# A new order string, a memset moved to a later step and stores by smaller pieces in a one-core attention and mixture-of-experts kernel

## The chip, the core and the metric

The kernel runs on one core of one Trainium2 chip. The metric is the device time of one execution in microseconds (us), lower is better. The kernel before was timed in three runs; their median is the number that the change is held against.

## The reference

The input is x with 4 batches of 1024 tokens of 128 features, in fp32. Two blocks follow each other, each added to its input (cut to what matters):

```
n = layernorm(x)
Q, K, V = silu(n@Wq), silu(n@Wk), silu(n@Wv)          # 8 heads of 16
scores = (Q K^T + rel_bias[i - j]) / 4, causal, keys that are all 0 masked
x = x + (silu(scores) @ V) * silu(n@Wu)               # no softmax
n = layernorm(x)
gates = softmax over the 2 largest of n@w_gate^T      # 8 experts
x = x + sum_e gates[e] * ((n @ w_in[e]^T) @ w_out[e]^T)
```

## The kernel before

**Work and groups.** The tokens are cut into groups: seven of 512 tokens (g0 to g6, four tiles of 128) and, at the end, two of 256 (g7 and g8). Groups 2b and 2b+1 belong to batch b; g7 and g8 are the second half of batch 3.

**An order written out by hand.** All instructions come from generators, and each `yield` ends a step. The string `ORDER` has 424 letters; each letter runs the next step of one lane, and the instructions of that step are queued on their engines (TensorE = PE, VectorE = DVE, ScalarE = ACT, GpSimd = POOL, SyncE = SP for DMAs) in the order in which they are written. Each engine works through its own queue in that order; an instruction that must wait holds up everything behind it on its engine, and no other engine. The lanes, with the names that the text uses for their steps:

- P and Q, `prepare`: the two halves of a batch, eight steps each. P1 to P3 make the normalised, transposed input; P4 the keys, P5 the queries, P6 the mask of keys, P7 the values (into `vps`), P8 U. For batch 0 (`layernorm_T`) P1 is statistics on DVE and a power on POOL, P2 the scaling, P3 PE transposes. For the others (`layernorm_cols`) P1 is the statistics, P2 is a transpose on DVE (L276) and three DMAs on SP that write the statistics to DRAM (L277) and read them back as rows for all partitions (L297, L301), and P3 two POOL operations (L305, L306).
- S, `attend`: one unit of scores of 512 columns. PE multiplies into four PSUM banks (L492), then DVE adds the relative bias (L511) and ACT applies silu (L514), or ACT does both where the bias is one constant (L519). The banks come from a ring of seven that nearly all PE work shares.
- W, `weigh`: the product of the oldest waiting unit with V (L470). The last W of a group starts its `finish`.
- C, D, E, `finish`: F1 transposes the result back, F2 to F4 are a layernorm like P1 to P3, F5 the gate logits, F6 to F14 choose two experts on small tiles, F15 writes the gates to DRAM and reads them back broadcast (L628), M0 to M3 multiply a tile of tokens by its eight gates (L635).
- X, Y, Z, `experts` for g0 to g6: X0 to X3, one tile each, 64 matmuls and one DVE addition (L650). For g7 and g8 `experts_then_gates`: for each of two tiles a and b are two products with ACT (L672) and DVE (L676), c three DVE additions (L683 to L685).
- G, `fold`: w_in times w_out of one expert. K, `constants`: K1 is the far bias, K2 and K3 the diagonal tiles of the bias (a POOL select L245 and a DVE copy L249), K4 a ranking, K5 the clearing of `vps[1]`.

Before the first letter, `load_all` issues the loads and the POOL memsets, among them the clearing of `vps[0]` (L169), V's room of batches 0 and 2, 128 x 2048 elements. On SP it loads x, the bias tables, and, behind a wait for a small table that goes through DRAM (`ext`), the rest of x and all expert weights.

**Stores.** `store` issues one DMA to `out` on SP. In `experts` it is called once for a group, after X3; in `experts_then_gates` once for a group, after its last tile.

Of the kernel before, what the change touches and what calls it, by code (L numbers as in the profile page):

```python
# [24 lines left out]
TPB = SB // P  # L25
# [15 lines left out]


ORDER = (
    "PPQPQKPPQKPKSPSPSQQSWWSWGSWQPWSQWSPSCSWQPSCCQKWGSPWPSWWSWPKQSWGSWSWSCWSWPSWPSGDSQQDPQWSCPP"
    "WWSWQWSQDWSSCESCDWPEPCSCWQWEDCSWPCSWCQDSWDCSWDDDCPGSPPWQCDSQWSWSGWESGWPSWSWSDEWECQEDPEDEEC"
    "GDQWWSXSWSQCXECSCEXSECQWSCEXPWPWSDEDQPCQWSDDWDSYDSWQEESWDCYCCYCDCSWWWESCYCSPCWCCSZDCQWSEDZ"
    "SDEWPEQQWSEZSDWWDQDCDQSDCDWZDSDCXCSEWEWEWCCESWEECXXEESQWDSEWDDXSEDEYCSEDDWWDSCCYDCCCSCDCDY"
    "CSCYCDWCDESDWWEDDSZDWWEDWDEYEEYEYYZECZEEECEYEECZXEYEXEEZCZZZXZXZ"
)


# [1 line left out]
def preln_silu_attention_moe(  # L53
# [14 lines left out]
    nc = tc.nc  # L68
# [19 lines left out]
    def misc():  # L88

        return ps_s.tile([P, SB], F32, tag="bank", name="bank")  # L90

    def product(out, stationary, moving, start=True, stop=True):


        for q in range(0, P, 32):
            nc.tensor.matmul(  # L96
                out[q : q + 32, :], stationary[:, q : q + 32], moving, start=start, stop=stop
            )
# [4 lines left out]
    def load_x(b, blk):  # L103
        t0 = blk * TPB
        nc.sync.dma_start(
            xs[b][:, t0 : t0 + TPB, :],
            x[b, blk * SB : (blk + 1) * SB, :].rearrange("(i p) d -> p i d", p=P),
        )
# [15 lines left out]
    def load_w(i, w):  # L124
        nc.scalar.dma_start(wcat[:, i, :], w)

    def load_near(par, to, src, pitch, n):
        nc.sync.dma_start(
            near[:, par, :, to : to + n],
            bass.AP(src.tensor, src.offset, [[1, P], [2 * pitch, NQ], [1, n]]),  # L130
        )

    def load_all():

        pt = misc()
        for i in range(HEAT):
            product(pt[:, :P], ident, ident)

        load_x(0, 0)
        nc.scalar.dma_start(rb[:, NPAD - NR :], rel_biasT)  # L140
        load_w(1, wk)
        load_near(0, FAR, rel_biasT, NR, MAXLEN)

        nc.vector.memset(one, 1.0)
        nc.scalar.activation(one, one, AF.Silu)
        nc.vector.tensor_copy(
            rb[:, : NPAD - NR], rb[:, NPAD - NR : NPAD - NR + 1].to_broadcast([H, NPAD - NR])
        )
        nc.scalar.dma_start(ext[:, :], rb)
        load_w(0, wq)  # L150
        load_x(0, 1)
        load_near(1, FAR, rel_biasT[1:2, :], NR, MAXLEN)

        load_near(0, FAR - P, ext[0:1, FAR - P :], NPAD, P)
        load_near(1, FAR - P, ext[1:2, FAR - P :], NPAD, P)
        load_w(2, wv)
        load_w(3, wu)
        nc.gpsimd.memset(wgT, 0.0)

        nc.gpsimd.memset(ones8, 1.0)  # L160
        nc.gpsimd.affine_select(
            out=ones8, in_=ones8, compare_op=ALU.is_ge, fill=0.0,
            base=0, pattern=[[-HD, H]], channel_multiplier=1,
        )
        nc.gpsimd.affine_select(
            out=ones8, in_=ones8, compare_op=ALU.is_ge, fill=0.0,
            base=HD - 1, pattern=[[HD, H]], channel_multiplier=-1,
        )
        nc.gpsimd.memset(vps[0], 0.0)  # L169
        nc.gpsimd.memset(euler, EULER)  # L170
        for st in stats:
            nc.gpsimd.memset(st, 0.0)
        nc.scalar.dma_start(wgT[:, :E], w_gateT)

        for n in range(2, B * NB):
            load_x(n // NB, n % NB)
        for e0 in range(0, E, 2):

            if e0 % 4 == 0:
                room = gpool.tile([P, 2, 2, 2, NC, D], F32, tag="wide", name=f"w_in_out_{e0}")  # L180
            both = room[:, e0 // 2 % 2]
            for t, w in zip((both[:, 0], both[:, 1]), (w_in, w_outT)):
                nc.sync.dma_start(t, w[e0 : e0 + 2].rearrange("e (c p) d -> p e c d", p=P))
            experts_in.append(both)
# [31 lines left out]
    vps = [cpool.tile([P, NT, 2, NQ, 2, HD], F32, tag=f"vp{i}", name=f"vp{i}") for i in range(2)]  # L216
# [9 lines left out]

    def constants():


        pt = misc()  # L230
        nc.tensor.matmul(
            pt[:, :H], rb[:, :1].to_broadcast([H, P]), ident[:H, :H], start=True, stop=True
        )
        for par in range(2):
            nc.scalar.copy(
                near[:, par, :, : FAR - P],
                pt[:, :H].rearrange("p (k q) -> p q k", q=2)[:, par, :]
                .unsqueeze(2).to_broadcast([P, NQ, FAR - P]),
            )
        nc.vector.tensor_scalar(cscaled, pt[:, :H], SCALE, None, ALU.mult)  # L240
        yield

        for par in range(2):
            diag = near[:, par, :, TAB - P : TAB]
            nc.gpsimd.affine_select(  # L245
                out=diag, in_=diag, compare_op=ALU.is_ge, fill=NEG,
                base=P - 1, pattern=[[0, NQ], [-1, P]], channel_multiplier=-1,
            )
            nc.vector.tensor_copy(near[:, par, :, TAB:], diag)  # L249
            yield  # L250

        nc.gpsimd.iota(
            rank, pattern=[[0, TPB], [-1, E]], base=E, channel_multiplier=0,
            allow_small_or_imprecise_dtypes=True,
        )
        yield
        nc.gpsimd.memset(vps[1], 0.0)
        yield
# [278 lines left out]
    def finish(g, b, t0, nt, gated):  # L537
# [82 lines left out]
        if g in DIRECT:  # L620
            lanes["XYZ"[g % 3]].append(experts_then_gates(b, t0, nt, x2T, gates))
            yield
            return
# [6 lines left out]
            gates_d[g].rearrange("r j -> (r j)").partition_broadcast(P),  # L630
        )
        lanes["XYZ"[g % 3]].append(experts(b, t0, wide_g))
        yield
        for i in range(nt):
# [5 lines left out]
    def experts(b, t0, gated):  # L640

        y = xs[b][:, t0 : t0 + TPB, :]
        for i in range(TPB):
            pt = misc()
            for e in range(E):
                product(
                    pt[:, :D], gated[:, i, e, :], wfold[:, e, :],
                    start=(e == 0), stop=(e == E - 1),
                )
            nc.vector.tensor_tensor(y[:, i, :], pt[:, :D], y[:, i, :], ALU.add)  # L650
            if i == TPB - 1:
                store(b, t0, TPB, y)
            yield

    def experts_then_gates(b, t0, nt, x2T, gates):

        EH = SB // D
        y = xs[b][:, t0 : t0 + nt, :]
        for i in range(nt):

            both = spool.tile([P, 2 * EH, D], F32, tag="both", name="both")
            gy, other = both[:, : EH + 1, :], both[:, EH + 1 :, :]
            for e0 in (EH, 0):
                pt = misc()
                product(
                    pt, x2T[:, i, :], wfold[:, e0 : e0 + EH, :].rearrange("p e d -> p (e d)")
                )
                for e in range(EH):
                    ye = pt[:, e * D : (e + 1) * D]
                    gate = gates[:, i, e0 + e : e0 + e + 1]  # L670
                    if e0:
                        nc.scalar.activation(  # L672
                            other[:, e, :] if e < EH - 1 else gy[:, EH, :], ye, AF.Copy, scale=gate
                        )
                    else:
                        nc.vector.scalar_tensor_tensor(  # L676
                            gy[:, e, :], ye, gate,
                            other[:, e, :] if e < EH - 1 else y[:, i, :],
                            ALU.mult, ALU.add,
                        )  # L680
                yield
            half = EH // 2
            nc.vector.tensor_tensor(gy[:, :half, :], gy[:, :half, :], gy[:, half:EH, :], ALU.add)  # L683
            nc.vector.tensor_tensor(gy[:, 0, :], gy[:, 0, :], gy[:, EH, :], ALU.add)
            nc.vector.tensor_tensor(y[:, i, :], gy[:, 0, :], gy[:, 1, :], ALU.add)  # L685
            if i == nt - 1:
                store(b, t0, nt, y)
            yield

    def store(b, t0, nt, y):  # L690
        nc.sync.dma_start(
            out[b, t0 * P : (t0 + nt) * P, :].rearrange("(i p) d -> p i d", p=P), y[:, :nt, :]
        )
# [10 lines left out]
    lanes["Q"] = [prepare(b, 1) for b in range(B)]  # L704
    lanes["G"] = [fold()]
    lanes["K"] = [constants()]

    def step(lane):
# [52 lines left out]
```

## Time and profile before

| | us |
|---|---|
| median of three runs | 277.42 |
| lowest and highest | 276.55, 277.86 |
| the profiled execution's own time | 276.35 |
| its span, from first to last instruction | 274.6 |
| PE busy in the span | 264.8 |
| DVE busy | 229.8 |
| ACT busy | 194.0 |
| POOL busy | 88.6 |

The profile is of one execution, 1.75 us shorter in span than in time. PE matmuls are pipelined and their ends are modelled, so a busy PE can still be slow inside; the starts of its instructions are exact. "Idle before" is time in which an engine did nothing before a group of instructions, and what it names is what ended the idle time. The TensorE clock was granted in full throughout (1.000).

### The profile page before, as it was taken

Reading aid. Unit: us, or ns where it says so; the run is one execution under the profiler, and the core shown is the slowest. Engines: PE = TensorE matmul, PEld = TensorE weight load, DVE = VectorE, ACT = ScalarE, POOL = GpSimd, SP = SyncE. Lnnn points to the kernel's source line nnn. Section 1 sums busy time; section 2 is a strip of 40 time slices with the busy share of each in tenths; the row PEclk is TensorE's granted clock in tenths of the full one; section 3 lists DMA queues with packets and bytes.
Section 4 is the critical chain, followed back from the end, with each engine's and each line's share of the span. In section 5 each row is a group of like instructions: output and inputs, shape, how many; then the busy total and the mean of one; then the engine's idle time right before and its main releaser. Section 6 shows DMA issues by size and latency. Waiting matters only on the chain.

```text
span 274.6 us, 10777 instructions
## 1 busy us (share of the span) xinstructions
PE 264.8 (96%) x4694; PEld 145.2 (53%) x4694; DVE 229.8 (84%) x594; ACT 194.0 (71%) x316; POOL 88.6 (32%) x101
## 2 busy tenths in 40 slices
PE   7799999999999999999999999999998999999993
PEld 7344443344444234444465347565675776775872
DVE  5597656569976977999989898999899998898994
ACT  2568998879899898889768866575965467684030
POOL 7410136600544712372024241351360343111010
PEclk9999999999999999999999999999999999999999
DMA  5899930330004032272080483217022621845022
GB/s 176 214 301 287 290 128 5 117 117 2 0 5 124 35 77 84 81 300 91 5 309 2 123 333 97 79 41 284 31 82 97 256 80 43 308 143 211 5 60 60
DMA packets 33315, 34.88 MB, mean 127 GB/s; under 512 B 4068, under 2 KB 29676, under 8 KB 32372
## 3 DMA queue, kind: packets, MB, share of 16 engines
q1 hardware_dynamic: 32516, 33.89, 38.3%
q8 instruction: 37, 0.61, 0.9%
q10 hardware_dynamic: 752, 0.31, 0.4%
q14 instruction: 10, 0.08, 0.1%
HBM read 31.74 MB, written 2.45 MB: 124 GB/s over the span
## 4 chain that ended last, share of the span: by engine, by line
PE 85%; DVE 8%; POOL 2%; issue 2%; ACT 1%; POOLq 0%; DVEq 0%
PE bank L96 31%; PE bank L492 29%; PE av L470 22%; DVE w L511 3%; DVE gated L635 2%; PE bank L541 2%; POOL rstd L325 1%; PE bank L569 1%; POOL vp L169 1%; DVE den L608 1%; ACT w L519 1%; DVE attended L479 0%; ACT w L514 0%; POOL xn L330 0%; DVE near L249 0%
## 5 line engine op out<-in xcount | busy, mean ns | idle before, releaser
L511 DVE TENSOR_TENSOR w<-bank,near 128x512 f32<-128x512 f32 (+2 forms) x220 | 116.5, 589 | 18.0 <-PE bank L492 15.0
L514 ACT ACTIVATE w<-w 128x1024 f32<-128x1024 f32 (+2 forms) x110 | 98.2, 915 | 40.5 <-DVE w L511 37.8
L492 PE MATMUL bank<-qT,kT 32*128 32x512 f32 (+3 forms) x864 | 91.0, 483 | 1.4 <-DVE x L650 0.8
L519 ACT ACTIVATE w<-bank,cscaled 128x512 f32<-128x512 f32 (+3 forms) x136 | 70.2, 604 | 10.4 <-PE bank L492 5.9
L470 PE MATMUL av<-w,vp 128*32 128x512 f32 (+3 forms) x864 | 74.0, 454 | 0.4 <-DVE turned L276 0.3
L492 PEld LDWEIGHTS bank<-qT,kT 32*128 32x128 f32 x864 | 39.7, 184 | 39.5 <-DVE w L511 14.9
L96 PE MATMUL bank<-wfold,gated 128*32 128x128 f32 x1792 | 53.9, 273 | 0.3 <-issue 0.3
L96 PEld LDWEIGHTS bank<-wfold,gated 128*32 128x32 f32 x1792 | 48.3, 110 | 9.2 <-issue 4.6
L470 PEld LDWEIGHTS av<-w,vp 128*32 128x32 f32 x864 | 23.2, 109 | 34.6 <-issue 26.3
L635 DVE TENSOR_TENSOR gated<-gated,x2T 128x1024 f32<-128x1024 f32 x28 | 35.8, 1288 | 0.9 <-DMA gated<-gates_d 0.9
L289 POOL TENSOR_TENSOR stats<-rs,mhalf 128x4 f32<-128x4 f32 x13 | 13.2, 1019 | 46.8 <-DVE rs L288 44.0
L96 PE MATMUL bank<-xnT,wcat 128*32 128x512 f32 x192 | 24.3, 597 | 0.5 <-ACT xnT L338 0.4
L605 POOL TENSOR_TENSOR ex<-euler,d 128x4 f32<-128x4 f32 (+1 forms) x9 | 9.6, 1061 | 41.0 <-DVE d L603 37.0
L406 POOL TENSOR_TENSOR vp<-v,kmask 128x256 f32<-128x256 f32 x16 | 9.8, 632 | 31.8 <-ACT v L404 31.8
L305 POOL TENSOR_TENSOR mean<-attended,mean 128x512 f32<-128x512 f32 x7 | 9.3, 1324 | 19.8 <-DMA mean<-stats_d 19.8
L672 ACT ACTIVATE both<-bank,gates 128x128 f32<-128x128 f32 x16 | 4.5, 375 | 14.9 <-DVE gates L619 11.0
L305 POOL TENSOR_TENSOR mean<-xT,mean 128x512 f32<-128x512 f32 x6 | 7.7, 1283 | 20.4 <-DMA mean<-stats_d 20.4
L96 PEld LDWEIGHTS bank<-xnT,wcat 128*32 128x32 f32 x192 | 5.3, 109 | 13.3 <-issue 5.2
L371 ACT ACTIVATE kT<-bank,sel 128x512 f32<-128x512 f32 x16 | 11.0, 690 | 0.2 <-PE bank L96 0.2
L306 POOL TENSOR_TENSOR x2T<-mean,x2T 128x512 f32<-128x512 f32 x7 | 9.8, 1402 | 0.6
L284 DVE BATCH_NORM_STATS2 stats<-x 128x6 f32<-128x256 f32 x26 | 9.8, 418 | 0.1
L96 PEld LDWEIGHTS bank<-w_in_out 128*32 128x32 f32 x256 | 7.0, 110 | 4.5 <-DVE w L511 2.4
(87 smaller groups left out, 204.4 us busy)
## 6 DMA issues: line engine op xcount, KB each, us to landing
gated<-gates_d SPq DMA_DIRECT2D x7, 2048.0 KB, 8.2
mean<-stats_d SPq DMA_DIRECT2D x13, 256.0 KB, 3.6
x<-in_L_attn_x SPq DMA_DIRECT2D x8, 256.0 KB, 6.4
w_in_out<-in_L_ffn_w_in SPq DMA_DIRECT2D x4, 512.0 KB, 7.4
w_in_out<-in_L_ffn_w_out SPq DMA_DIRECT2D x4, 512.0 KB, 7.5
xT<-in_L_attn_x_T SPq DMA_DIRECT2D x8, 256.0 KB, 4.4
x2T<-stats_d SPq DMA_DIRECT2D x7, 256.0 KB, 3.7
out<-x SPq DMA_DIRECT2D x7, 256.0 KB, 2.3
```

Of the source, the lines that this page charges most:

```text
L96: nc.tensor.matmul(out[q : q + 32, :], stationary[:, q : q + 32], moving, start=start, stop=stop)
L284: nc.vector.bn_stats(st[:, 3 * i : 3 * i + 6], src[:, i : i + 2, :].rearrange("p i d -> p d i"))
L289: nc.gpsimd.tensor_tensor(st[:, TPB * 3 : TPB * 4], rs, mhalf, ALU.pow)
L305: nc.gpsimd.tensor_tensor(mean, srcT, mean, ALU.subtract)
L306: nc.gpsimd.tensor_tensor(dst, mean, dst, ALU.mult)
L371: nc.scalar.activation(kT[:, par, s0 : s0 + SB], pk, AF.Silu, scale=sel[:, par : par + 1])
L470: nc.tensor.matmul(acc[k * 32 : (k + 1) * 32, nt * P - n : nt * P], vp[:, j, par, k, :, :].rearrange("p q c -> p (q c)"), w[:, k, c : c + ...
L492: nc.tensor.matmul(ps[k][:, c : c + n], kT[k * 32 : (k + 1) * 32, par, j * P : (j + 1) * P], qT[k * 32 : (k + 1) * 32, lo : lo + n], start ...
L511: nc.vector.tensor_tensor(w[:, k, :nn], ps[k][:, :nn], near_of(k, parts), ALU.add)
L514: nc.scalar.activation(w[:, k : k + 2, :nn], w[:, k : k + 2, :nn], AF.Silu, scale=SCALE)
L519: nc.scalar.activation(w[:, k, lo:hi], ps[k][:, lo:hi], AF.Silu, bias=cscaled[:, h : h + 1], scale=SCALE,)
L635: nc.vector.tensor_tensor(wide_g[:, i], wide_g[:, i], x2T[:, i : i + 1, :].to_broadcast([P, E, P]), ALU.mult)
```

## The change

The clearing of `vps[0]` is no longer issued in `load_all`, but as the first instruction of K1. `experts` stores after X1 and after X3, two tiles each time; `experts_then_gates` stores every tile by itself. `ORDER` is a different string with the same 424 letters, each letter as often as before; 85 of the 424 places hold the same letter. The computation and its instructions stay the same, but for nine more stores.

```diff
 ORDER = (
-    "PPQPQKPPQKPKSPSPSQQSWWSWGSWQPWSQWSPSCSWQPSCCQKWGSPWPSWWSWPKQSWGSWSWSCWSWPSWPSGDSQQDPQWSCPP"
...
-    "CSCYCDWCDESDWWEDDSZDWWEDWDEYEEYEYYZECZEEECEYEECZXEYEXEEZCZZZXZXZ"
+    "PPQQPKKPQPQQPKSPSSSWPSGWSWPWQPSQWPSWSCWCQSPPQSKCWWSCWWPSWSSWCQSWSWQKSWSWPCSWPSGWSCQQSDPWWD"
...
+    "DCDYSDCYCDEWESDWESWDDEWWZDWYEEYEYZECZEEECEYEEXEYEZEEYZCZCZZZXZXX"
 )
...
-        nc.gpsimd.memset(vps[0], 0.0)
         nc.gpsimd.memset(euler, EULER)
...
     def constants():
 
+        nc.gpsimd.memset(vps[0], 0.0)
 
         pt = misc()
...
-            if i == TPB - 1:
-                store(b, t0, TPB, y)
+            if i % 2:
+                store(b, t0 + i - 1, 2, y[:, i - 1 :])
             yield
...
-            if i == nt - 1:
-                store(b, t0, nt, y)
+            store(b, t0 + i, 1, y[:, i:])
             yield
```

More of the change, by code (lines that the diff above doesn't have):

```diff
@@ L43 @@
 ORDER = (
-    "PPQPQKPPQKPKSPSPSQQSWWSWGSWQPWSQWSPSCSWQPSCCQKWGSPWPSWWSWPKQSWGSWSWSCWSWPSWPSGDSQQDPQWSCPP"
-    "WWSWQWSQDWSSCESCDWPEPCSCWQWEDCSWPCSWCQDSWDCSWDDDCPGSPPWQCDSQWSWSGWESGWPSWSWSDEWECQEDPEDEEC"
-    "GDQWWSXSWSQCXECSCEXSECQWSCEXPWPWSDEDQPCQWSDDWDSYDSWQEESWDCYCCYCDCSWWWESCYCSPCWCCSZDCQWSEDZ"
-    "SDEWPEQQWSEZSDWWDQDCDQSDCDWZDSDCXCSEWEWEWCCESWEECXXEESQWDSEWDDXSEDEYCSEDDWWDSCCYDCCCSCDCDY"
-    "CSCYCDWCDESDWWEDDSZDWWEDWDEYEEYEYYZECZEEECEYEECZXEYEXEEZCZZZXZXZ"
+    "PPQQPKKPQPQQPKSPSSSWPSGWSWPWQPSQWPSWSCWCQSPPQSKCWWSCWWPSWSSWCQSWSWQKSWSWPCSWPSGWSCQQSDPWWD"
+    "SPWSWGPSDCWQSEWSDQECPCPSWEQGCQDSWSCDGCCWSWPDCDQSDDWWSEWEEEPDSWSPWDSGWDSGCWDGSXDQSCWQQCSWXE"
+    "WPESCWCEESCXPWSWQPDDECWSEXECDEQDYWSDYDSYCCQQCSCCWCSCWDPPECQSWWPESEDWPCSYDWCCQSWSEWDQQWDSWD"
+    "SDZWDCZESEPZSDWSDXSWWDEQQCDSWZDCCSWSECWECSEEEXCESWEEXWDWQESDWSDYDXCCEESCEDCDCWSWDCYDCSCDDC"
+    "DCDYSDCYCDEWESDWESWDDEWWZDWYEEYEYZECZEEECEYEEXEYEZEEYZCZCZZZXZXX"
 )
```

## The prediction

> **What bounds the kernel now.** I read the page's busy line first, then the chain of waits, the groups by form, the waits, and last the timeline at both ends and around the first batch change. PE is busy nearly throughout, and the chain that ended last lies on PE from 13 us on:
>
> ```profile
> span 274.6 us, 10777 instructions
> PE 264.8 (96%) x4694; PEld 145.2 (53%) x4694; DVE 229.8 (84%) x594; ACT 194.0 (71%) x316; POOL 88.6 (32%) x101
> PE 85%; DVE 8%; POOL 2%; issue 2%; ACT 1%; POOLq 0%; DVEq 0%
> ```
>
> But busy is not full speed. From the starts of matmuls in the timeline I took what each step costs when nothing holds it (lower quarter of its kind): an S step 1.07 us, a W step 0.88, an expert tile of 64 matmuls 1.77, a projection 0.86 to 0.90. All steps: 73 S and 73 W make 142, 28 expert tiles 49, the projections 29, fold, direct products, transposes and logits 24, in all 243.9 us. The first transpose starts at 7.39 and the last matmul ends at 270.39: 263.0. So some 19 us are PE held up, 11 of them in sixteen steps that each took over 0.25 us too long. Both strings hold the same steps; the order can touch only those 19 us, the 7.4 before and the 4.2 behind.
>
> What holds PE is the ring of seven banks, emptied by DVE and ACT:
>
> ```profile
> L511 DVE TENSOR_TENSOR w<-bank,near 128x512 f32<-128x512 f32 x156 | 95.9, 680 | 11.4 <-PE bank L492 11.2
> L514 ACT ACTIVATE w<-w 128x1024 f32<-128x1024 f32 x78 | 82.1, 1058 | 40.5 <-DVE w L511 37.8
> L635 DVE TENSOR_TENSOR gated<-gated,x2T 128x1024 f32<-128x1024 f32 x28 | 35.8, 1288 | 0.9 <-DMA gated<-gates_d 0.9
> ```
>
> Started back to back, an addition takes 0.60 us, a silu of 1024 columns 0.96, a gate multiplication 1.12. An S step with four additions costs DVE 2.4 us for PE's 1.07; such steps must be spread between steps that are PE's alone.
>
> **The tail.** The chain's last pieces:
>
> ```profile
> 255.31 15.08 PE bank L96 x440
> 270.39 0.02 issue
> 270.41 0.29 DVE x L650
> 270.70 0.34 DVE both L683
> ...
> 271.14 0.30 DVE both L684
> 271.44 0.02 issue
> 271.47 0.29 DVE x L685
> ```
>
> PE runs without a gap to 270.39, X3 of g6. Behind it DVE does X3's addition and then the three of g8's last tile (letter Z), to 271.76; the last store and its landing take the rest to 274.6. The new string ends XX, with that Z ahead of both: three additions, 1.06 us (271.76 less 270.70), go before the last matmul. Is DVE then late by itself? In the window 250 to 275 it is busy 19.92 us and has almost no gap from 250.2 to 269.9. But M3 of g5 (1.12) and F14 of g7 (0.26) now stand ahead of the last W, not behind it: DVE has 1.4 us less to do after that W. So X3 stays PE's, and the tail gives **-1.06**.
>
> **The start.** The lines that carry it:
>
> ```profile
> 1.80 1.80 POOL L169 MEMSET vp<- 128x2048 f32 x1
> 2.48 1.58 DVE L146 COPY rb<-rb 8x256 f32<-8x256 f32 x1 [1.57 <-DMA rb<-in_L_attn_rel_bias]
> 7.77 0.76 DVE L316 BATCH_NORM_STATS2 st<-x 128x6 f32<-128x256 f32 x2 [0.67 <-DMA x<-in_L_attn_x]
> 10.79 1.22 POOL L245 TENSOR_SCALAR_AFFINE_SELECT near<-near 128x512 f32<-128x512 f32 x2
> 10.93 0.66 PE L337 MATMUL bank<-ident,xn 128*128 128x128 f32 x4
> ```
>
> The memset ends at 3.60, and POOL then idles 1.10 until DVE's statistics: nothing on POOL waited for it. Its cost may be on DVE: the copy of 256 elements took 1.58 us beside it, while the same operation on 512 (L249) took 0.83 and 0.41. The Trainium skill, SBUF — State Buffer, section "SBUF: two separate sides", says that DVE and GpSimd share a port pair as an exclusive lock held for a whole instruction. By that rule the copy would end 1.2 us sooner, and so would the small table, the loads behind it, and P1: up to -1.2. By the row, the second half of x lands at 7.77 whatever DVE does, and the steps behind it set when scores start. I take 0 at the start. In its new place the memset stands on POOL after Q's scaling (10.82): 10.8 to 12.6, and delays the two selects and the copy by 1.8. That copy then ends near 14.1 instead of 12.29. In the new string the queries come after Q3's transposes (10.93), so the second half of the keys is ready near 13.9 anyway: 0.2 is lost at most, and the first scores start near 14.9 instead of 13.21 with 1.8 us more of projections done (5.5 instead of 3.7 us of PE work). Bounds -1.2 to +1.8, value 0.
>
> **Stores.** Nine more on SP:
>
> ```profile
> L691 SPq DMA_DIRECT2D out<-x x9: 372/389/425, 153.6 to 271.8; - x9
> DMA to landing us min/median/max: 2.3/2.3/2.3
> ```
>
> That is 9 x 0.39 = 3.5 us of SP, which issues little after 60 us. A store waits for an addition that DVE does before any transpose that a later SP transfer needs, so it holds nothing up. Against splitting speaks the Trainium skill, DMA: Bandwidth & Descriptors, section "Anatomy of one DMA": a fixed cost of about 2.0 us each (fitted on the GpSimd path). Nine of those in a row would be 18 us; by the row they overlap other work, and only the last landing counts, which is of two tiles before and after. Value 0; ends -0.3 (less queued behind) and +0.4 (one issue more).
>
> **The order inside.** I walked along both strings with a balance: each step adds its DVE (and, in a second balance, ACT) time and takes off its PE time, never below zero. What exceeds 4 us counts as PE waiting: seven banks are 1.75 S steps, at 2.4 us of DVE each. Before: 3.5 us (M0 and M1 of g0, M3 of g1, M1 of g3). After: 2.0, of which 1.6 in the opening, where S steps come three in a row. With limits of 3.5 and 4.5 it is 7.8 to 5.7 and 2.0 to 1.1. I take **-1.5**; ends +1 and -3, since the balance finds only part of the 19.
>
> **Leads.** The layernorms through DRAM have a latency of their own. The first:
>
> ```profile
> 33.20 0.67 SPq L277 DMA_DIRECT2D stats_d<-turned  x1
> 36.36 0.38 SPq L297 DMA_DIRECT2D mean<-stats_d  x1
> ...
> 40.35 1.27 POOL L305 TENSOR_TENSOR mean<-xT,mean 128x512 f32<-128x512 f32 x1 [4.36 <-DMA mean<-stats_d]
> 41.69 1.29 POOL L306 TENSOR_TENSOR xnT<-mean,xnT 128x512 f32<-128x512 f32 x1
> ```
>
> DVE's transpose ended at 33.17, POOL at 42.98: 9.8 us; the others took 7.9 to 9.3 where POOL was free. Before, P4 of this half came at 44.5, 1.5 us later than needed. In the new string P2 comes earlier (18.3 instead of 23.1 us of PE work) but finds SP still issuing expert weights and x transposed until 31.6, so the keys' input is ready near 42.6, while PE reaches P4 (27.6 us of work, about 12.4 behind the clock) near 40. It stands 2.6 us. ACT, which is busy 26.7 of the 30 us from 32 to 62 and paces that stage, loses only about 1.6, and part returns by the second group: **+0.7**. Other leads shrink too, in PE work between transpose and use: g5 13.9 to 9.1, g4 16.0 to 10.3, batch 2 first half 12.2 to 10.4, g0 32 to 9.7. With DVE 0.3 to 2.5 us behind PE there (the balance), most just hold: **+0.3**.
>
> **Sum.** -1.06 + 0 + 0 - 1.5 + 0.7 + 0.3 = -1.6. The profiled execution took 276.35 (span 274.6 and 1.75 around it), 1.07 below the median; I take the difference from the median: 277.42 - 1.6 = 275.8.
>
> **Rivals.**
> - The balance is half of it: the new string also spreads what the balance doesn't see, and saves 3 us inside. For: 11 us sat in single steps. Against: the opening packs five S steps closer. -3.1: 274.3. Chance 0.18.
> - Slower by late layernorms: DVE runs 2 to 3 us behind PE where the new leads are shortest (as it did at batch 2's P2, 3 us). Then PE stands at P4 of batch 1 in full (2.6), and, at a lag of 3, at F5 of g5 (9.05 + 3 - 9.1 = 3), of g0 (8.1 + 3 - 9.7 = 1.4) and at batch 2's P4 (8.7 + 3 - 10.4 = 1.3); behind each, S steps and their DVE and ACT work start late. At a lag of 2 us it is 2.6 + 2.0 + 0.4 + 0.3 = 5.3; less the tail's 1.06 and the balance's 1.5 that leaves +2.7: 280.1. It decides from where the waits pass 2.6 us in sum, which P4 alone reaches if nothing of it returns. Chance 0.23.
> - The parts cancel: the first batch's loss eats the tail's gain, the balance means nothing. 277.4. Chance 0.12.
>
> **How the numbers follow.** About 0.5%, 1.4 us, is what a measurement of this kernel can tell from no change. My forecast has 0.47 (own range 274.6 to 276.9), 0.29 of it beyond 0.5%. Faster 0.29 + 0.18 = 0.47; same 0.18 + 0.12 = 0.30; slower 0.23. The range 273.0 to 279.4 leaves out the ends of the first two rivals, somewhat under 2 in 10.
>
> **What would show it.** Tail: X3's addition is the last DVE instruction, 0.3 us after the last matmul. Start: L146 well under 1 us, scores from about 14.9. First batch change: PE stands before P4's product near 40 to 43. Inside: fewer S steps far over 1.07 us. Wrong: PE waiting for POOL x2T L306 or xnT at several places, or a last matmul later than 270.4.

## The result, and the profile after

The changed kernel took 280.53 us in the median of 22 runs, the kernel before, run beside it, 276.97: a ratio of 1.0116 (95% interval 1.0089 to 1.0142). It is slower by 1.2%, and above the range predicted. The ratio leaves out runs over 1.5% above their kernel's fastest, six of the changed kernel's 22 and its first traced execution among them, so the lines of "after" are of a later execution of the same kernel (280.37 us, span 278.7; that set of runs gave 1.0123, 1.0079 to 1.0166). In its code L228 is the moved memset and L690 the store.

The head of the page of after, and its chain:

```profile
span 278.7 us, 10800 instructions
PE 268.3 (96%) x4694; PEld 147.1 (53%) x4694; DVE 232.5 (83%) x594; ACT 194.6 (70%) x316; POOL 90.5 (32%) x101
PE 79%; DVE 10%; ACT 5%; issue 3%; POOL 2%; DVEq 0%; POOLq 0%
```

PE is busy 3.5 us longer with the same instructions, and 6% of the chain have gone from PE, most of it to ACT and DVE. Between the first transpose and the last matmul PE needs 243.9 us of undisturbed steps in both kernels; what it takes beyond that I call its excess, whether PE waits, runs slowly or is at half clock. It was 19.1 us before and is 23.9 here.

**The opening.** The timeline of after (start, duration, instruction, idle time before it):

```profile
3.16 0.28 DVE L146 COPY rb<-rb 8x256 f32<-8x256 f32 x1 [2.25 <-DMA rb<-in_L_attn_rel_bias]
...
9.78 2.76 DVE L330 TENSOR_SCALAR xn<-x,st,rstd 128x128 f32<-128x128 f32 x3 [1.15 <-POOL rstd L325]
...
10.61 1.93 DVE L240 TENSOR_SCALAR cscaled<-bank 128x8 f32<-128x8 f32 x1
10.66 1.80 POOL L228 MEMSET vp<- 128x2048 f32 x1
...
12.60 0.47 PE L337 MATMUL bank<-ident,xn 128*128 128x128 f32 x1 [1.39 <-DVE cscaled L240]
```

L146 is free of the memset and takes 0.28 us instead of 1.58. The price stands below: the memset follows POOL's own scaling at once, and DVE's third scaling (inside the 2.76 us) lasts until it ends, 2.18 us where it took 0.44 before. L240, of 8 columns, stands behind that scaling on DVE and ends with it (1.93, before 0.18). The last of Q3's transposes, which needs the third scaling, waits 1.39 us; the profile names L240, which ended at the same time. The same stretch by windows of 2 us (busy time of PE, PEld, DVE, ACT, POOL, then the granted clock):

```profile
10.00:12.00 2.00, 0.79 (x7) 0.34 (x3) 2.00 (x4) 0.69 (x1) 2.00 (x2) 1.00 0.67 144
12.00:14.00 2.00, 1.41 (x9) 0.53 (x13) 1.37 (x3) 0.59 (x1) 1.65 (x3) 0.65 1.01 267
14.00:16.00 2.00, 2.00 (x16) 0.45 (x12) 0.00 (x0) 1.00 (x2) 0.00 (x0) 0.50 1.20 314
16.00:18.00 2.00, 2.00 (x36) 0.69 (x28) 1.21 (x3) 1.54 (x4) 0.00 (x0) 1.00 1.19 288
```

After the gap PE runs at half clock until 16.01 us: products of 0.86 us take 1.71. The first scores start at 17.26 us, against 13.21 before. Not all of that stays lost. The keys of batch 1 (P4) wait in the new order for their input, which a layernorm through DRAM brings:

```profile
42.64 1.92 PE L96 MATMUL bank<-xnT,wcat 128*32 128x512 f32 x16
```

The input was ready at 42.59. With the memset in its old place (a_memset_back, below) PE stands 1.60 us there and starts at 42.22. In these two executions, then, only 0.4 us of what the memset does to the opening reaches beyond P4.

**Inside.** Near 104 us, the layernorm of g2 and the mask of keys of batch 2 (P6, L387), timeline of after:

```profile
104.34 1.28 POOL L305 TENSOR_TENSOR mean<-attended,mean 128x512 f32<-128x512 f32 x1 [3.22 <-DMA mean<-stats_d]
104.39 1.28 DVE L587 TENSOR_TENSOR oh<-lg,m 128x32 f32<-128x32 f32 x1
...
105.70 1.27 POOL L306 TENSOR_TENSOR x2T<-mean,x2T 128x512 f32<-128x512 f32 x1
105.77 1.25 DVE L616 TENSOR_TENSOR oh<-oh,g 128x32 f32<-128x32 f32 x1
...
107.16 0.69 DVE L387 TENSOR_TENSOR nz<-kT 128x512 bf16<-128x512 f32 x1
...
107.90 0.26 PE L96 MATMUL bank<-ones,nz 128*32 128x8 bf16 x16 [1.72 <-DVE nz L387]
```

L587 and L616 took 0.19 and 0.18 us in the median before. Each started just after a POOL instruction and ended with it; the two lost 2.2 us, L387 came late, PE stood 1.72. The windows behind it again show half clock:

```profile
104.00:108.00 4.00, 2.28 (x43) 0.79 (x40) 3.75 (x9) 3.78 (x8) 2.55 (x2) 1.00 0.24 83
108.00:110.00 2.00, 2.00 (x24) 0.57 (x22) 1.01 (x7) 0.00 (x0) 0.00 (x0) 0.54 0.05 8
110.00:112.00 2.00, 2.00 (x16) 0.52 (x16) 1.83 (x4) 0.45 (x1) 0.00 (x0) 0.60 0.51 131
```

Instructions of DVE that lie beside such a POOL instruction and are over 0.15 us longer than their kind: about 10 before, 6.6 us too long in sum; about 14 after, 10.4 us (L240 counted).

**The tail and the stores.** The chain's last pieces, and the stores' line:

```profile
274.69 0.30 DVE both L684
274.99 0.02 issue
275.02 0.29 DVE x L685
275.31 0.48 DVE x L650 x2
```

```profile
L690 SPq DMA_DIRECT2D out<-x x18: 332/386/392, 139.8 to 275.8; - x18
DMA to landing us min/median/max: 1.5/2.5/6.5
```

The last matmul ends at 275.43, X3's addition is the last thing DVE does, and the span ends 3.2 us after the matmul instead of 4.3.

### The profile page after: what moved, and what is told of

It reads as the page before. It is cut to its first block, busy times and chain, and to the rows that moved or that the text cites. A ratio compares the mean times of both kernels' runs of the same rounds, so it can differ in the third digit from the quotient of the medians.

```text
span 281.6 us, 10800 instructions
## 1 busy us (share of the span) xinstructions
PE 270.6 (96%) x4694; PEld 147.3 (52%) x4694; DVE 232.5 (83%) x594; ACT 194.7 (69%) x316; POOL 90.9 (32%) x101
## 3 DMA queue, kind: packets, MB, share of 16 engines
HBM read 31.74 MB, written 2.45 MB: 121 GB/s over the span
## 4 chain that ended last, share of the span: by engine, by line
PE 77%; DVE 8%; DMA 5%; ACT 5%; SPq 2%; issue 1%; DVEq 0%
PE bank L96 27%; PE bank L492 25%; PE av L470 22%; ACT w L519 3%; DVE w L511 3%; DMA w_in_out<-in_L_ffn_w_out 3%; DMA ext<-rb 2%; SPq L105 2%; ACT w L514 2%; PE bank L541 2%; DVE gated L635 1%; DMA rb<-in_L_attn_rel_bias 1%; DVE both L676 1%; SPq L128 1%; DVE gates L619 1%
## 5 line engine op out<-in xcount | busy, mean ns | idle before, releaser
L519 ACT ACTIVATE w<-bank,cscaled 128x512 f32<-128x512 f32 (+3 forms) x136 | 70.0, 611 | 10.3 <-PE bank L492 8.8
L470 PE MATMUL av<-w,vp 128*32 128x512 f32 (+3 forms) x864 | 76.7, 465 | 0.0
L289 POOL TENSOR_TENSOR stats<-rs,mhalf 128x4 f32<-128x4 f32 x13 | 13.6, 1045 | 61.8 <-DVE rs L288 44.6
L96 PE MATMUL bank<-xnT,wcat 128*32 128x512 f32 x192 | 26.6, 657 | 0.4 <-ACT xnT L338 0.4
L605 POOL TENSOR_TENSOR ex<-euler,d 128x4 f32<-128x4 f32 (+1 forms) x9 | 10.5, 1162 | 25.8 <-DVE d L603 25.8
L305 POOL TENSOR_TENSOR mean<-attended,mean 128x512 f32<-128x512 f32 x7 | 9.7, 1393 | 20.8 <-DMA mean<-stats_d 20.8
L96 PEld LDWEIGHTS bank<-xnT,wcat 128*32 128x32 f32 x192 | 6.3, 119 | 13.8 <-issue 7.3
L305 POOL TENSOR_TENSOR mean<-xT,mean 128x512 f32<-128x512 f32 x6 | 7.7, 1284 | 17.1 <-DMA mean<-stats_d 17.1
L291 POOL TENSOR_TENSOR attended<-attended,xT 128x512 f32<-128x512 f32 x7 | 9.4, 1342 | 0.0
```

The source lines that it names most:

```text
L96: nc.tensor.matmul(out[q : q + 32, :], stationary[:, q : q + 32], moving, start=start, stop=stop)
L289: nc.gpsimd.tensor_tensor(st[:, TPB * 3 : TPB * 4], rs, mhalf, ALU.pow)
L305: nc.gpsimd.tensor_tensor(mean, srcT, mean, ALU.subtract)
L470: nc.tensor.matmul(acc[k * 32 : (k + 1) * 32, nt * P - n : nt * P], vp[:, j, par, k, :, :].rearrange("p q c -> p (q c)"), w[:, k, c : c + ...
L519: nc.scalar.activation(w[:, k, lo:hi], ps[k][:, lo:hi], AF.Silu, bias=cscaled[:, h : h + 1], scale=SCALE,)
L605: nc.gpsimd.tensor_tensor(ex, euler[:, :nt], d, ALU.pow)
```

## The experiments

Ratios are to the kernel before, run on the same chip, with the 95% interval.

**The parts by themselves.** The new string and stores, memset in its old place (a_memset_back):

```diff
+        nc.gpsimd.memset(vps[0], 0.0)     # in load_all, where it was
...
-        nc.gpsimd.memset(vps[0], 0.0)     # in K1
```

> New order and new stores, the clearing of vps[0] back in load_all. Theory lock: the three L330 of Q2 take 1.0 us together, Q3's transposes start near 11.0, no half clock in the first 25 us, 3 to 4.5 us less than the changed kernel: ratio to before 0.995 to 1.002. Theory order: nothing of note returns, ratio to before 1.008 to 1.014; L146 is again 1.58 us.

The old kernel with only the memset moved to K1 (b_memset_k1), and with only the new stores (b_stores):

> Old order and old stores, the clearing of vps[0] at K1. Theory lock: K1 follows Q2 in the old order too, so L330 of Q2 is held as well, Q3's transposes start near 13 instead of 10.93, PE idles some 2 us and may lose its clock: 2 to 4.5 us more than before, ratio 1.007 to 1.016. Theory order: within 0.4% of before, since nothing waits on POOL there.

> Old order, old place of the memset, new stores (two tiles, or one). Theories lock and order: within 0.3% of before, as 9 more issues of 0.39 us stand on a queue that is mostly idle. A theory that the stores cost: SP's issues push a layernorm's transfers or the broadcast of gates back, ratio 1.004 or more.

The changed kernel once more (a_again), on the same chip:

> The changed kernel once more, for a second trace and a time beside the others. Theory lock (the memset of vps[0], now at K1, holds DVE's scaling of the second half of x through the port that DVE and POOL share; PE then idles over 1 us and runs at half clock for some us): L330 of Q2 takes over 2 us again, the granted clock falls below 1 before 25 us, ratio to before 1.010 to 1.015. Theory order (the loss lies in the new order of steps, wherever the memset is): the same ratio, but the opening ends (first W, g0.0) less than 2 us later than before's for the PE work done by then, and the loss lies later.

Measured: a_memset_back 1.0091 (1.0061 to 1.0121), b_memset_k1 1.0086 (1.0060 to 1.0111), b_stores 0.9995 (0.9972 to 1.0017). The stores cost nothing that shows. The memset alone, and the string with the stores, each cost nearly a percent, and all together only 1.2%: on top of the string the memset adds 0.25%, uncertain by 0.4. Timeline of b_memset_k1, the old string:

```profile
10.72 2.76 DVE L330 TENSOR_SCALAR xn<-x,st,rstd 128x128 f32<-128x128 f32 x3 [1.16 <-POOL rstd L325]
...
11.61 1.80 POOL L228 MEMSET vp<- 128x2048 f32 x1
...
13.54 0.33 PE L337 MATMUL bank<-ident,xn 128*128 128x128 f32 x1 [1.39 <-DVE cscaled L240]
```

It is the same picture as in after, so the place of the memset makes it, not the string. In a_memset_back there is no such gap (0.92 us remain), and PE waits later instead, at P4 of batch 1's first half:

```profile
42.22 1.92 PE L96 MATMUL bank<-xnT,wcat 128*32 128x512 f32 x16 [1.60 <-POOL xnT L306]
```

In after PE comes to this product later by more than that (42.64) and does not wait. So most of what the opening wins is waited away at P4, which fits that the parts don't add up.

**Other places and shapes of the memset**, in the old kernel: eight memsets of 256 elements at K1 (b_memset_pieces), and one in K3, behind the second select (b_memset_k3).

```diff
+        for i in range(NT):
+            nc.gpsimd.memset(vps[0][:, i], 0.0)
```

> Old order and stores, the clearing of vps[0] at K1 but as eight memsets of 256 elements instead of one of 2048. Theory lock (what holds DVE is one long POOL instruction that has the shared port until it ends): the third L330 of Q2 waits for one piece at most (0.3 us), Q3's transposes start before 11.7 instead of 13.2, and most of the 0.86% of the single memset at K1 is gone: ratio 0.998 to 1.004. Rival (POOL's queue is what is late: the selects of K2 behind the same 1.8 us of memset): ratio stays 1.006 to 1.011.

```diff
+            if par == 1:
+                nc.gpsimd.memset(vps[0], 0.0)
```

> Old order and stores, the clearing of vps[0] after the second select, in K3, where DVE's scaling of x is over and POOL has nothing until V. Theory lock: at most the small copy L249 of K3 is held; ratio 0.997 to 1.003, against 1.0086 at K1. Rival (any later place costs, since V's product waits for POOL): ratio 1.004 or more.

Measured 1.0145 (1.0106 to 1.0185) and 1.0071 (1.0040 to 1.0101); both theories were wrong (for K3 the rival's number came, not its reason). Timeline of the pieces (lines are one further down in this kernel), then of K3:

```profile
10.08 3.03 DVE L331 TENSOR_SCALAR xn<-x,st,rstd 128x128 f32<-128x128 f32 x3 [1.16 <-POOL rstd L326]
...
10.96 2.07 POOL L229 MEMSET vp<- 128x256 f32 x8
```

```profile
11.48 2.58 DVE L250 COPY near<-near 128x512 f32<-128x512 f32 x1 [0.55 <-POOL near L244]
11.98 1.80 POOL L249 MEMSET vp<- 128x2048 f32 x1
...
14.70 0.27 PE L96 MATMUL bank<-ones,nz 128*32 128x8 bf16 x16 [2.61 <-DVE nz L388]
```

DVE does not get in between POOL instructions that follow each other at once: its third scaling, within the 3.03 us, takes 2.45 beside eight short ones, and 2.18 beside one long one. In K3 it is the bias copy that is held (2.58 us, before 0.83), by a select and then the memset, and P6's mask behind it keeps PE waiting 2.61 us.

**The clock.** The changed kernel, with 8 unneeded products of 128x128 ahead of Q3's transposes (a_warm), and with 8 more ahead of the mask of batch 2 (a_warm2):

```diff
+        for i in range(warm):
+            product(pt[:, :P], ident, ident)
```

> The changed kernel with eight unneeded 128x128 products on PE ahead of Q3's transposes, in the time in which PE otherwise stands for DVE. Theory clock (the wait costs twice: PE's idle time, and then a granted clock of a half for some 3.4 us): the clock stays 1.00 from 8 to 20 us, and the ratio to before falls from 1.012 to 1.005 to 1.009. Rival (in the opening DVE and ACT set the pace, a slow PE costs nothing): ratio stays 1.010 to 1.015.

> The changed kernel with eight unneeded products ahead of Q3's transposes, as before, and eight more ahead of the small product of P6 of batch 2, where PE stands 2 to 3 us for DVE. Theory clock: no half clock after 105 us, ratio from 1.003 to 0.998 to 1.002. Rival (the half clock inside is covered by DVE and ACT, which set the pace there): 1.002 to 1.005.

Measured: a_warm 1.0028 (1.0005 to 1.0050), a_warm2 1.0076 (1.0051 to 1.0100). Timeline and window of a_warm:

```profile
13.07 0.33 PE L339 MATMUL bank<-ident,xn 128*128 128x128 f32 x1 [1.39 <-DVE cscaled L240]
```

```profile
14.00:16.00 2.00, 2.00 (x20) 0.52 (x16) 0.73 (x2) 1.56 (x4) 0.12 (x1) 1.00 1.16 310
```

The gap is the same 1.39 us, and the clock behind it stays at 1.00 (in this execution behind the wait at 106 us too). Over all runs the mean clock is 0.989 in after, 0.995 in a_memset_back, and 0.997 to 0.999 in a_warm, a_warm2 and before. So the clock was mended in both kernels, but a_warm gains 0.9% on after and a_warm2 only 0.4%, uncertain by 0.4 each. What eight more products cost in a_warm2, and why a_warm beats a_memset_back, I can't explain. By these two, a third to three quarters of the loss would be the clock's. Of after's executions in the ratio, the eleven with a mean clock of 0.992 or more took 279.14 us in the median, the five with 0.982 to 0.988 took 280.97. Without the clock's worst, then, some 2 us of the loss remain.

When the clock falls can be read from the traces. In each of them all changes lie whole multiples of 3.41 us apart; in after half clock runs from 12.60 to 16.01 and from 108.17 to 111.58. PE's busy time in the stretch ahead of each fall, then around the longest wait of b_memset_k3 (the number behind the five engines is the clock):

```profile
9.19:12.60 3.41, 1.61 (x12) 0.35 (x4) 2.76 (x4) 1.38 (x3) 3.31 (x4) 1.00 0.66 142
104.76:108.17 3.41, 1.69 (x40) 0.62 (x36) 3.06 (x6) 3.02 (x7) 2.13 (x2) 1.00 0.07 25
```

```profile
10.15:13.56 3.41, 1.95 (x16) 0.58 (x12) 2.86 (x5) 2.54 (x5) 3.41 (x4) 1.00 0.95 254
13.56:16.97 3.41, 2.27 (x56) 1.29 (x56) 2.53 (x6) 0.00 (x0) 0.22 (x1) 1.00 1.20 298
```

In the twenty traces there are fourteen falls. Ahead of twelve PE was busy 0.25 to 0.58 of such a stretch, ahead of two 0.85, which I can't explain; no stretch below 0.52 kept the full clock, and between 0.53 and 0.58 some did. In b_memset_k3 a stop of 2.61 us is cut in two by the end of a stretch, PE is busy 0.57 and 0.67 of the two, and the clock stays. So the same stop can cost half clock in one execution and not in another.

**Single waits taken out of the new string** (memset in its old place in all four). a_p6_early has the mask of batch 2 five letters earlier, a_f3_late has F3 of g2 eleven places later, a_best has that and 4 products ahead of Q3's transposes, a_p4_late has P4 and P5 of batch 1 behind four and six other PE steps:

```diff
-"...QDSWSCDGCCWSWPDCDQ..."
+"...QDSWSCDGPCCWSWDCDQ..."                       (a_p6_early)
-"SPWSWGPSDCWQSEWSDQECPCPSWEQGCQDSWSCDGCCWSW..."
+"SPWSWGPSDCWQSEWSDQECPCPSWQGCQDSWSCDGECCWSW..."   (a_f3_late, a_best)
-"...SCWCQSPPQSKCWWSCWWPSWS..."
+"...SCWCQSQSKCWWPSCWPWPSWS..."                   (a_p4_late)
```

> New order and stores with the memset back in load_all, and one letter moved: P6 of batch 2's first half (DVE's not_equal and the small product on PE) comes five letters earlier, ahead of F13 and F14 of g0. Theory lock inside: there F13 and F14 of g0 are held 2.2 us by the two POOL operations of g1's layernorm (L305, L306), the not_equal stands behind them on DVE and PE behind that, idle near 105; with P6 ahead the step W g3.5 loses its 1.8 us, and the ratio falls from 1.009 to 1.000 to 1.005. Rival (DVE's work is late in any case, and the wait moves to the next S step): 1.007 to 1.011.

> New order and stores with the memset back in load_all, and one letter moved: F3 of g2 (the transpose and the DMAs of its statistics) comes after G4 instead of before P8 of batch 1, some 4 us later, so that L305 and L306 of g2 run after P6 of batch 2 and not beside F13 and F14 of g0. F5 of g2 had 5.8 us to spare. Theory lock inside: L614 and L619 of g0 take 0.2 us each, the step W g3.5 loses its 1.8 us of wait and no half clock follows: ratio from 1.009 to 1.001 to 1.005. Rival (DVE is late there by its load alone, or the hold only moves): 1.007 to 1.011.

> New order and stores, memset back in load_all, F3 of g2 later as in a_f3_late, and four unneeded products ahead of Q3's transposes. Theory (locks at two places and the clock behind them explain the loss): below 1.000, by the tail's 1 us perhaps 0.996. Rival (the new order has more waits of its own, such as the S steps of the opening): 1.002 to 1.006.

> The new string with the memset in its old place, where P4 and P5 of batch 1's first half are moved behind four and six other steps of PE's (two W and an addition-heavy S go ahead of P4). Theory 'what the opening wins is lost at P4': PE no longer waits there (1.67 us with the memset back, nothing with the memset at K1), and what was won stays won, in part: the excess at place 60 falls from 8.8 to about 7.3 us, ratio 1.003 to 1.006. Rival: the wait turns up at the next late input (P5's or P6's, or S of g2), or DVE is late by then anyway; ratio 1.007 to 1.012.

Measured 1.0235 (1.0199 to 1.0271), 1.0105 (1.0077 to 1.0132), 1.0115 (1.0064 to 1.0165) and 1.0220 (1.0168 to 1.0273): none gained. Timelines, in that order (a_best is left out):

```profile
104.27 1.76 DVE L387 TENSOR_TENSOR nz<-kT 128x512 bf16<-128x512 f32 x1
...
106.08 0.27 PE L96 MATMUL bank<-ones,nz 128*32 128x8 bf16 x16 [3.06 <-DVE nz L387]
```

```profile
42.44 2.81 PE L96 MATMUL bank<-xnT,wcat 128*32 128x512 f32 x16 [2.50 <-POOL xnT L306]
```

```profile
43.23 1.13 PE L492 MATMUL bank<-qT,kT 32*128 32x128 f32 x10 [0.93 <-ACT w L519]
```

In a_p6_early the mask itself now starts beside L305 and is held. In a_f3_late the wait at 104 us is gone as expected, but PE, 0.7 us earlier in the opening of this execution, waits 2.50 at P4, and the layernorm that was moved now comes too late for its own use: ahead of F5 of g2 PE stands 1.10 us for x2T (1.55 in a_best).

```profile
113.50 0.43 PE L569 MATMUL bank<-x2T,wgT 128*32 128x128 f32 x8 [1.10 <-POOL x2T L306]
```

So this edit exchanges one wait for another, and does not show what the wait at 104 us is worth. In a_p4_late P4 no longer waits, but the two projections had been PE's work between two S units; without them PE waits for a bank that ACT still reads (L519), and two steps there take 2.2 and 1.8 too long, the second for P6's mask.

**The tail's letters alone** (b_tail): old string, new stores, last two letters exchanged.

```diff
-"...ZECZEEECEYEECZXEYEXEEZCZZZXZXZ"
+"...ZECZEEECEYEECZXEYEXEEZCZZZXZZX"
```

> Old order with new stores and the last two letters exchanged, ZX instead of XZ: the three additions of g8's last tile stand on DVE ahead of X3's. The tail as the prediction had it: the last DVE instruction ends 0.3 us after the last matmul and not 1.4, ratio 0.996 (0.994 to 0.998) against 0.9995 without the exchange. Rival (DVE is itself late at the end, the additions only push X3's back): 0.998 to 1.001.

Measured 1.0018 (0.9992 to 1.0045). In its trace the last matmul ends at 270.66 and the last addition at 271.60: with the old letters ahead of them, the three additions make DVE late, and X3's has to wait for them.

**The two strings cut and joined.** At places 304 and 356 both strings have used the same letters, so that one can go on where the other stops; at 58 they differ by a C and a G, and these two were put right in the rest. h_old356 takes the new letters only from place 356, h_old304 from 304, h_old58 from 58; h_new58 is the old string behind the new 58 letters. Memset in its old place and new stores in all.

```diff
+ORDER = OLD[:356] + NEW[356:]      # in effect; and so on
```

> The old string up to place 356, the last 68 letters of the new one (M3 of g5 and F14 of g7 now ahead of the last W, and the three additions of g8 ahead of the last X). The tail's term, by itself: the end comes 0.9 to 1.1 us after the last matmul's end sooner than before (3.3 us instead of 4.2), PE's excess in the last 68 letters is 0.7 before and 0.9 to 1.8 in the new string, 0.2 to 1.1 more. Theory 'the tail's gain is real by itself': ratio 0.996 to 0.999. Rival, 'it is given back ahead of it, at X3 of g4 and the last units of g8': 0.999 to 1.002.

> The old string up to place 304, the new one behind it; memset in its old place. Theory 'middle' (the loss lies at places 58 to 304): only the late part's own excess is left, 3.8 us against 3.4 before, with the wait at X3 of g4 (0.8 to 1.6), less the tail's 0.9: ratio 0.997 to 1.000. Rival 'late' (the loss is X3 of g4 and what leads to it): 1.002 to 1.005.

> The new string with the memset in its old place, but its first 58 letters are those of the old string (with F4 of g0 behind them and G1 left out of the rest, so that every letter comes as often as before). Theory 'opening': PE's excess up to that place was 5.9 us in the kernel before and 7.4 in the new string with the memset back, and the half clock that follows the waits there goes too. The excess falls by 1.5 to 2.5 us, ratio 0.999 to 1.004. Rival 'late': the loss is the wait at W of g3 near 104 us with the half clock behind it, and the steps after; then the ratio stays at 1.006 to 1.010, and the first 58 letters are worth nothing.

> The counterpart: the old string and memset with the first 58 letters of the new one (G1 behind them, F4 of g0 left out of the rest). Theory 'opening': S units 2 and 3 of g0 again take 1.2 us too long each, P4 of batch 1 waits 1.5 to 2.5, and the loss appears without any of the later letters: ratio 1.004 to 1.009. Rival 'late': 0.998 to 1.002.

| kernel | new letters from place | ratio | PE's excess up to place 29, 60, 140, 304, the end (us, one execution) |
|---|---|---|---|
| before | none | 1 | 3.7, 5.9, 11.1, 15.7, 19.1 |
| h_old356 | 356 | 0.9972 (0.9949 to 0.9996) | 4.0, 6.2, 10.9, 15.6, 19.3 |
| h_old304 | 304 | 1.0041 (1.0017 to 1.0065) | 4.0, 6.2, 11.6, 17.2, 21.5 |
| h_old58 | 58 | 1.0043 (1.0020 to 1.0065) | 4.0, 6.6, 12.9, 17.0, 20.8 |
| a_memset_back | 0 | 1.0091 (1.0061 to 1.0121) | 5.0, 8.8, 13.6, 17.2, 21.0 |
| after | 0, and the memset | 1.0116 (1.0089 to 1.0142) | 6.9, 9.3, 16.1, 20.8, 23.9 |

The excess is of one execution each, up to 2.1 us off its kernel's median (that of a_memset_back is its fastest run): it shows where time goes, the ratio how much. Ratios read from row to row, each difference uncertain by 0.3 to 0.4%: the last 68 letters gain 0.28%, letters 304 to 356 lose 0.7% (1.9 us), letters 58 to 304 nothing, the first 58 lose 0.5% (1.3 us), the memset 0.25%, which may be nothing. h_new58, with 1.0055 (1.0022 to 1.0089), confirms the opening's share from the other side. h_old356 is faster than the kernel before (276.50 against 277.05 us in the median), though its interval only just leaves out 1. Its end, in the timeline:

```profile
265.80 4.55 PE L96 MATMUL bank<-wfold,gated 128*32 128x128 f32 x160
...
270.15 0.56 DVE L650 TENSOR_TENSOR x<-bank,x 128x128 f32<-128x128 f32 x2
```

Last matmul at 270.35, last addition at 270.71, span 273.6, against 270.35, 271.76 and 274.6 before.

What letters 304 to 356 do is seen best in h_old304, at X3 of g4, PE's timeline:

```profile
237.13 1.93 PE L96 MATMUL bank<-wfold,gated 128*32 128x128 f32 x64
...
240.07 0.64 PE L96 MATMUL bank<-wfold,gated 128*32 128x128 f32 x15
...
242.10 1.58 PE L96 MATMUL bank<-wfold,gated 128*32 128x128 f32 x49 [1.40 <-issue]
```

PE stops for 1.40 us in the middle of one tile, where it waits for no data. The stop is in before too, at the same matmul, but short:

```profile
239.82 1.58 PE L96 MATMUL bank<-wfold,gated 128*32 128x128 f32 x49 [0.31 <-issue]
```

The DMA view of h_old304 from 239.5 to 240.7 us shows what lands there:

```profile
q1 hardware_dynamic: 273, 0.17, 47.2%
q8 instruction: 1, 0.02, 5.7%
```

A packet of 16 KB of the queue "instruction" runs from 239.54 to 240.64, just behind the 2 MB broadcast of g5's gates, whose packets fill the engines from 234.0 to 239.6; in before the corresponding one starts at 237.46, and PE goes on 1.4 us after it has landed, as here. That PE runs out of instructions because their transfer comes late was not tried by itself, but the place of the stops speaks for it. Over the twenty traces PE stops 18 times for over 0.2 us with no wait named. Counting all of PE's recorded instructions from the start (matmuls, weight loads and some 30 waits), 14 of these stops follow the 7873rd, two the 6849th, one each the 7105th and 8129th: always whole multiples of 256 apart. In a_warm the added products shift the count by 128, and X3 of g4 runs through; PE stands 1.05 us behind its 8129th instead, at a unit of g8, though there the profile names ACT. In a_warm2 they shift the count by 256, and the stop is back in X3 of g4 (0.82 us). X3 of g4 is 0.1 to 0.95 us too long in the eight traces with the old letters from 304 to 356 (mean 0.5), 0.75 to 1.6 in the ten with the new ones and the count not shifted by 128 or 64 (mean 1.25). That would be some 0.8 of the 1.9 us; the rest is open.

Last, F3 of g2 moved as in a_f3_late, in h_old58 (h_old58_f3):

> The new string with the old first 58 letters, and F3 of g2 moved behind G4, eleven places later. Theory: with the old opening the removed wait is not given back at P4 or in half clock, so PE's 1.8 us at W of g3 and what the clock loses there are won: 1.0043 becomes 0.997 to 1.001. Rival: the layernorm meets DVE's instructions at another place (W of g3's next unit took 1.3 too long when F3 was moved in the whole new string), and the ratio stays at 1.002 to 1.006.

Measured 1.0073 (1.0039 to 1.0108). The wait at 104 us is gone, but 1.23 us stand ahead of F5 of g2 again, for the x2T of the layernorm that was moved, and no time is won, with the old opening either.

## Why the prediction was wrong

- **Tail, -1.06: right.** From the last matmul to the end it is 1.06 us less, X3's addition is last, and h_old356 gains 0.28% (0.8 us). The reason given, that M3 of g5 and F14 of g7 go ahead of the last W, fits: b_tail lacks it, DVE is late, and nothing is gained.
- **Stores, 0: right.** 0.9995; the 18 issues take 0.386 us each in the median and hold nothing up.
- **Order inside, -1.5: wrong in sign, and the largest failed step.** With the leads' +1.0 the working gave the new letters -0.5 us apart from the tail. Measured with the memset back they cost 0.91%, 2.5 us, although the tail gains 0.8: some +3.3. The balance found the opening (1.6 us there): two S steps (units 2 and 3 of g0) take 1.17 us each too long, where units 1 and 2 took 0.41 and 0.71 before. The reduction elsewhere did not come: S units 9 and 11 of g1 are 1.3 and 0.7 too long (0.4 and 0.9 before), and at 104 and 240 us PE stops for reasons that no balance of busy times contains, DVE held by POOL, and in all likelihood PE without instructions.
- **Start, 0: wrong, the second failed step.** L146 became short as the port rule said, and won nothing. The working let the memset delay only what stands behind it on POOL, two selects and a copy, "0.2 is lost at most". That part came as predicted: the copy ends at 13.93, predicted 14.1. What was left out is a scaling on DVE ahead of Q3's transposes, which is held to the memset's end. Alone in the old order that makes 0.86% (2.4 us); in the new order, where P4 waits in any case, 0.25%, which may be nothing. I had weighed the port for the old place and not asked the same question of the new one. The rule stands in the Trainium skill, SBUF — State Buffer, "SBUF: two separate sides": the pair is held for a whole instruction and the other engine blocks fully. The trace agrees (2.18 us beside a memset of 1.80), and the pieces show that the hold outlasts one instruction.
- **The clock, put at nothing.** Every term was costed at full clock, since before shows 1.000. In the traced execution of after two stretches of 3.41 us ran at half clock; by that duration each costs up to 1.7 us where nothing else waits, my estimate, and less where P4 waits behind it. The skill's page TensorE: Matmul & The Clock Gate, Part 1, gives a window of about 3.4 us and half rate after an idle one. The traces agree on the length; but PE was busy 1.61 and 1.69 us of the two stretches ahead of the falls, so a half-idle one is enough here.
- **Leads, +0.7 and +0.3: the mechanism was there.** Predicted was a stand of 2.6 us at P4; it is 0.6 to 3.0 in the five kernels with the new opening and the memset back (a_p4_late, which moves P4, left out), and 0 in after, where PE is later.
- **The rival "slower by late layernorms"** had the right sign and nearly the right time, 280.1, by luck: of its four waits only the one at P4 shows in a_memset_back (1.60 us), and none in after. Layernorms cost there by holding DVE's instructions, not by PE waiting for x2T.

What stays open: the clock's share, the rest of what letters 304 to 356 lose, and why the first 58 letters cost 1.3 us in the runs when single executions show them 1.3 to 2.9 us worse in excess.

## What to carry to other kernels

A long POOL instruction that is moved must be laid against DVE's queue at its new place, not only against what follows on POOL; cutting it into pieces that follow at once does not help. On a kernel where PE is busy 96%, one wait seen in a trace is no estimate of what its removal brings, since PE may meet the next late input earlier (P4 here), and a moved step may come late for its own use (F5 here): exchange whole stretches of the order and measure those. If the tail of a new order is good and the rest is not, take the tail.

## What the runs showed of the hardware that I had not expected

- POOL holds DVE over back-to-back instructions: eight memsets of 0.31 us, one every 0.26, made a scaling that took 0.44 us before last 2.45 us.
- All changes of PE's clock within an execution lay multiples of 3.41 us apart. In twelve of fourteen falls to half PE had been busy 0.25 to 0.58 of the stretch just over, so it matters where a stop lies; a stop of 2.61 us that two stretches shared left the clock at 1.00.
- PE stopped 0.2 to 1.4 us amid work whose operands are all there, always a multiple of 256 of PE's instructions apart. Around X3 of g4 it went on 1.1 to 1.6 us after a 16 KB transfer of the instruction queue had landed.
